# Gates, in_proj and ssm_out as 32x32 tiles in one block of a scan kernel

## The chip, the cores and the metric

The kernel runs on one core of one Trainium2 chip. The metric is the time of one execution on the device, in microseconds. A core has TensorE (PE in the profile; its weight loads are PEld), VectorE (DVE), ScalarE (ACT), GpSimd (POOL) and SyncE (SP), which issues most transfers. Each runs its own list of instructions in order and waits on semaphores for the others. All arithmetic here is in f32.

## The reference

The input is x, 4 images of 128 channels and 96 x 96 points. It is normalized in 32 groups of channels, put through the layer below, and added to the result. The layer reads each image as a sequence of 9216 points in four ways: by rows, by rows backwards, by columns, by columns backwards. Each sequence goes through the same scan, and a 1x1 convolution (fuse_w) joins the four results:

```python
t = _grouped1x1(x, in_proj_w, in_proj_b, G)            # 4 groups of 32 channels -> 512
u, gate = (t[:, :HID], t[:, HID:])                     # 256 each
u = jax.nn.silu(u)
u = depthwise_conv(u, dw_w)                            # 5 taps, 256 channels
s = _conv1x1(u, ssm_in_w)                              # 32 channels each, from 256
a = DMIN + (DMAX - DMIN) * jax.nn.sigmoid(_conv1x1(u, ssm_delta_w, ssm_delta_b))
bb = jnp.tanh(_conv1x1(u, ssm_b_w, ssm_b_b))
cc = jnp.tanh(_conv1x1(u, ssm_c_w, ssm_c_b))
prefix = jnp.cumsum(jnp.log(a), axis=-1)
hst = jnp.exp(prefix) * jnp.cumsum(bb * s * jnp.exp(-prefix), axis=-1)
u = u + _conv1x1(cc * hst + ssm_d[None, :, None] * s, ssm_out_w)
u = _grouped1x1(u * jax.nn.sigmoid(gate), mix_w, mix_b, G)
return _conv1x1(u, out_proj_w, out_proj_b)
```

## The kernel before

**Units.** The work is 8 phases, for each of the 4 images first "V" (columns) and then "H" (rows). A phase runs a sequence and its reverse side by side. It has 6 steps of 16 lines. A step's 1536 points are held as 4 interleaved sets of N = 384 points (p = 0 to 3), so that neighbours along the sequence lie in neighbouring sets. A unit is one set of one direction, and a pair t holds the two directions' units of one set (s = 0 and 1): 24 pairs a phase, 192 in all. `pair(t)` records what the engines do for a pair. The order is written out by hand; no scheduler changes it.

**What a pair does**, by functions:
- `front` (`compute_front`, `in_proj`, `silu`): the grouped projection to u of a pair four ahead (t + 4), as 16 matmuls of 32 rows x 32 columns into four PSUM banks, then a silu per bank. In the second half of a phase the reversed sequence meets the same points, so the silu's results are kept in HBM and loaded again. Fronts are thus computed in pairs with t mod 24 in 20 to 23 and 0 to 7.
- `conv` and `conv_less`: the depthwise convolution of the first 128 channels as banded matmuls, 8 of 128 x 32 and 8 of 64 x 32, then a copy to u. `taps`: the other 128 channels, the first tap on ScalarE and four on VectorE, gathered in PSUM banks 0 and 1.
- `proj`: the projections to s, a, b and c, 16 matmuls of 128 x 32, then tanh and copies on ScalarE and two products on GpSimd. `scan` on VectorE and `outputs` on GpSimd make the value that goes into ssm_out, some pairs later.
- `out_of` (ssm_out): for the pair n = t - 6 (LAG = 6; its first unit is bi), four matmuls of 32 rows x 128 columns into banks 0 to 3. With `under`, ScalarE first lays u into the bank, so that the sum is made in PSUM; in the other pairs VectorE adds u.
- `gate` and `sigmoids`: the gates of pair n, four matmuls of 32 x 128 and four tanh (the factor of a half is folded into weights). The mirrored second half of a phase needs no new gates: they are kept in SBUF (`gates`, two tiles) and HBM (`kept`), and `load_kept` loads them. Gates are computed where n mod 24 is under 12, that is t mod 24 in 6 to 17.
- `gating` on VectorE multiplies, and `accumulate` applies the joined output weight W (w_fin: out_proj, mix and fuse in one, made at the start), 8 matmuls of 128 x 32 per unit; ScalarE copies the bank to `ys`, GpSimd adds it into `acc`.

In the profile an f32 matmul is two MATMUL records and two LDWEIGHTS. All matmuls recorded by the helper `mm` have its line, 134; the full-width gates are line 491, ssm_out line 504.

**Order.** A pair with kept gates runs on TensorE: in_proj, convolution, W (both units), less, ssm_out, projections. A pair with gates and no front: convolution, half of W, less, half of W, gates and ssm_out mixed (`gates_and_out`), projections. Two pairs of a phase have a front and gates, two have neither. TensorE has 8 PSUM banks: 0 to 3 for ssm_out (0 and 1 for the taps before that), and 4 to 7 are handed round among convolution, W, in_proj, gates and projections.

**Statistics.** In V phases, `stats_finish` works out the next image's normalization in pieces, one `next` in some pairs, with a few tiny matmuls (`product`).

**Transfers.** SyncE issues them in program order: the input x_in for fronts (`load_front`) and gates (`load_gate`), kept silus and gates, chunks for the statistics, the output, and the next image into acc.

Of the kernel before, what the change touches and what calls it, by code (L numbers as in the profile page):

```python
# [42 lines left out]
F32 = mybir.dt.float32  # L43
# [4 lines left out]
P = 128  # L48
# [8 lines left out]
R = 4  # L57
# [4 lines left out]
LAG = 6  # L62
# [5 lines left out]
def conv_preact_kernel(  # L68
# [111 lines left out]
    def stats_finish(b):  # L180
# [5 lines left out]

        mv = sp.tile([P, 2], F32, tag="mv", name=f"mv_{b}")
# [5 lines left out]
        nc.vector.tensor_copy(mean, pm[:, 0:1])  # L193
        dev = sp.tile([P, 1], F32, tag="dev", name=f"dev_{b}")
# [12 lines left out]
        nc.vector.tensor_scalar_add(var, pv[:, 0:2], GN_EPS)  # L207
        inv = sp.tile([P, 2], F32, tag="inv", name=f"inv_{b}")
        if b == b0:
            std = sp.tile([P, 2], F32, tag="err", name="std")  # L210
            nc.scalar.activation(std, var, AF.Sqrt)

            nc.scalar.activation(first_table, std[:, 0:1], AF.Silu)
            nc.vector.reciprocal(inv, std)
        else:
            bits = inv.bitcast(I32)
            nc.vector.tensor_single_scalar(bits, var.bitcast(I32), 1, ALU.logical_shift_right)
            nc.vector.tensor_scalar(bits, bits, -1.0, float(0x5F3759DF), ALU.mult, ALU.add)
            err = sp.tile([P, 2], F32, tag="err", name=f"err_{b}")
            for turn in range(3):  # L220
                if turn:
                    yield
                nc.gpsimd.tensor_mul(err, inv, inv)
# [3 lines left out]
        yield  # L227
        wns = sp.tile([P, 2, P], F32, tag="wn", name=f"wn_{b}")
# [16 lines left out]
        else:  # L245
# [3 lines left out]
            nc.vector.tensor_copy(shift, pb[:, 0:1])  # L249
            nc.vector.tensor_scalar_mul(spread, gmask, shift)  # L250
# [4 lines left out]
            nc.vector.tensor_sub(bn[:, 4:8], b_in[:, 4:8], pq[:, 0:4])  # L255
        nc.vector.tensor_scalar_mul(bn[:, 2:4], bn[:, 2:4], 0.5)
# [42 lines left out]

    b0 = phases[0][0]  # L300
# [7 lines left out]
    w_out_fuse = load(fuse, "fuse")  # L308
# [11 lines left out]
    w_mix = w_out_fuse[:, HID + 4 * P :].rearrange("p (j c) -> p j c", j=2)  # L320
# [140 lines left out]
    def in_proj(step, g, s, j, bk):  # L461
        wn = stats[units[step * UB]["b"]][0]
        r = slice(64 * s + 32 * j, 64 * s + 32 * j + 32)
        for c in range(4):
            m, q = (c, g) if j else (g, R - 1 - c if s else c)
            mm(bank(bk), c, wn[r, s, 32 * m : 32 * m + 32], x_in[s][r, q, :], True, True)

    def silu(step, g, s, j, bk):
# [3 lines left out]
            bank(bk)[:, : N + 1],  # L472
            AF.Silu,
# [19 lines left out]

    turning = (6, 0, 2)
# [11 lines left out]

    seeded = set()

    def under(bi, s):

        seeded.add(bi)
        nc.scalar.copy(psum[:, ssm(bi, s) : ssm(bi, s) + 2, :N], us[bi][:, s])  # L512

# [19 lines left out]

    def load_kept(n):
        m = mirror(n)
        if n < NU // 2 - R and m is not None and m < NP // 2 - 2:
            old_gates[n] = gates[m % 2]
            nc.sync.dma_start(old_gates[n], kept[n // NP % 2][m])
# [43 lines left out]
    def gating(bi, s):  # L582
# [3 lines left out]
        if m is None:  # L586
            g = gates[bi // 2 % 2][:, s]
        else:
            g = old_gates.get(bi // 2, gates[m % 2])[:, 1 - s, :, ::-1]
# [29 lines left out]
    def conv_less(i, banks):  # L619
# [10 lines left out]
        else:  # L630
            nc.scalar.copy(us[i][:, :, 0, :], psum[:, b0 : b0 + 2, :N])  # L631

# [291 lines left out]

    def tail():
# [90 lines left out]
    def start():  # L1016
        w_of = wp.tile([P, 4, 2, P], F32, name="w_of")

# [92 lines left out]
    with tc.manual_schedule(  # L1111
# [5 lines left out]
        for t in range(NU // 2):  # L1117
            pair(t)
        tail()
# [81 lines left out]
```

## Time and profile before

| | |
|---|---|
| runs shown | 1810.45, 1811.15, 1817.87 us; median 1811.15 |
| profiled execution, first to last instruction | 1812.7 us |
| TensorE busy | 1788.9 us, 24090 matmul records |
| weight loads | 645.3 us, 24090 |
| VectorE, ScalarE, GpSimd busy | 1446.5, 1567.0, 1432.0 us |
| granted TensorE clock, mean | 0.998 |
| transfers | 321.17 MB, mean 177 GB/s |

The page states for the profiled execution only its span, 1812.7 us; it is 1.55 us above the median of the runs. In a group's row, the line of the kernel, the engine, the operation, what is written and read with its shape and count come first, then busy time and mean ns of one, then the idle time ahead of these instructions and what ended it. In the timeline a row has start, length and count of like instructions that follow each other. In the table of stretches, "(x n)" counts the instructions that run in a stretch, also those that began before it.

### The profile page before, as it was taken

The numbers are of one execution on the slowest core, as the hardware profiler recorded it, in microseconds if no ns is written. First come the engines' busy times: TensorE is split into PE (matmuls) and PEld (weight loads), VectorE is DVE, ScalarE is ACT, GpSimd is POOL, SyncE is SP. The second block draws the span as 40 slices with busy tenths as digits, with TensorE's granted clock in tenths as the row PEclk, the third lists the DMA queues.
The fourth block names the chain that finished last, engine by engine and source line by source line (L and its number), as shares of the span: only waits on it lengthen the run. The fifth ranks groups of instructions, "written<-read, shape, count | busy, mean of one in ns | idle before, by whom it ended". The sixth has DMA issues, their size and how long they took to land.

```text
span 1812.7 us, 56970 instructions
## 1 busy us (share of the span) xinstructions
PE 1788.9 (99%) x24090; PEld 645.3 (36%) x24090; DVE 1446.5 (80%) x1462; ACT 1567.0 (86%) x2750; POOL 1432.0 (79%) x1477
## 2 busy tenths in 40 slices
PE   6999999999999999999999999999999999999998
PEld 3333333333333333333333333333333333333333
DVE  5888878887888887877788888787877878777886
ACT  4988888998888888898988888889888888889975
POOL 3587887778778888788877888778778788887876
PEclk9999999999999999999999999999999999999999
DMA  7655463444975466344696447443477734645434
GB/s 229 183 184 196 149 185 117 163 145 142 305 246 188 159 177 204 102 145 141 204 306 225 159 161 211 138 146 119 160 232 223 249 118 150 192 122 176 148 112 175
DMA packets 148047, 321.17 MB, mean 177 GB/s; under 512 B 14160, under 2 KB 115920, under 8 KB 147792
## 3 DMA queue, kind: packets, MB, share of 16 engines
q1 hardware_dynamic: 147648, 317.48, 54.4%
q8 instruction: 190, 3.11, 0.7%
q14 instruction: 65, 0.53, 0.1%
q10 hardware_dynamic: 144, 0.04, 0.0%
HBM read 185.21 MB, written 132.25 MB: 175 GB/s over the span
## 4 chain that ended last, share of the span: by engine, by line
PE 95%; DMA 2%; DVE 2%; ACT 1%; issue 0%; SPq 0%; DVEq 0%
PE psum L134 82%; PE psum L504 8%; PE psum L491 5%; DVE psum L650 1%; DMA x_in<-in_xs 1%; DMA xs<-in_xr 1%; DMA acc<-in_xr 0%; DVE u L597 0%; DVE u L650 0%; ACT psum L512 0%; PE psum L1035 0%; ACT u L631 0%; SPq L296 0%; ACT ys L757 0%; DVE bn L387 0%
## 5 line engine op out<-in xcount | busy, mean ns | idle before, releaser
L650 DVE SCALAR_TENSOR_TENSOR psum<-sil,small,psum 128x768 f32<-128x768 f32 x576 | 589.0, 1023 | 28.4 <-ACT psum L648 3.4
L597 DVE SCALAR_TENSOR_TENSOR u<-gate,psum 128x768 f32<-128x768 f32 x376 | 350.0, 953 | 273.4 <-ACT u L629 119.0
L134 PE MATMUL psum<-u,w_fin 128*32 128x384 f32 (+1 forms) x6192 | 551.1, 485 | 1.6 <-ACT ys L755 1.2
L134 PE MATMUL psum<-u,main 128*32 128x384 f32 x6144 | 534.7, 489 | 1.5 <-DVE u L650 1.4
L774 POOL TENSOR_TENSOR acc<-ys,acc 128x384 f32<-128x384 f32 x375 | 411.6, 1119 | 24.0 <-ACT ys L757 7.9
L728 POOL TENSOR_TENSOR t<-t,t 64x384 f32<-64x384 f32 (+1 forms) x192 | 237.7, 1238 | 156.9 <-DVE t L722 73.2
L134 PEld LDWEIGHTS psum<-u,w_fin 128*32 128x32 f32 x6192 | 189.3, 109 | 319.6 <-issue 215.3
L134 PEld LDWEIGHTS psum<-u,main 128*32 128x32 f32 x6144 | 181.9, 109 | 324.7 <-issue 197.2
L512 ACT COPY psum<-u 128x768 f32<-128x768 f32 x352 | 277.3, 801 | 17.5 <-DVE u L650 11.5
L134 PE MATMUL psum<-sil,band 128*32 128x384 f32 x3072 | 285.1, 488 | 0.0
L695 POOL TENSOR_SCALAR t<-tm 64x384 f32<-64x384 f32 x191 | 176.9, 926 | 117.3 <-ACT tm L687 97.9
L729 POOL TENSOR_TENSOR t<-t,t 64x384 f32<-64x384 f32 (+1 forms) x192 | 249.1, 1297 | 15.0
L504 PE MATMUL psum<-t,main 32*128 32x384 f32 x1536 | 238.6, 513 | 1.3 <-ACT psum L512 0.6
L648 ACT ACTIVATE psum<-sil,small 128x768 f32<-128x768 f32 x191 | 173.7, 909 | 56.2 <-DVE u L597 48.0
L521 ACT ACTIVATE gate<-psum,bnorm 128x384 f32<-128x384 f32 x384 | 192.2, 584 | 26.5 <-PE psum L491 25.5
L696 POOL TENSOR_TENSOR t<-t,tm 64x384 f32<-64x384 f32 x192 | 195.3, 1017 | 15.3
L650 DVE SCALAR_TENSOR_TENSOR u<-sil,small,psum 128x768 f32<-128x768 f32 x192 | 194.9, 1015 | 7.8
L470 ACT ACTIVATE sil<-psum,bnorm 128x385 f32<-128x385 f32 x384 | 192.6, 585 | 7.1 <-PE psum L134 4.8
L134 PE MATMUL psum<-sil,less 64*32 64x384 f32 x3072 | 168.1, 495 | 0.0
L491 PE MATMUL psum<-x_in,wn 32*128 32x384 f32 x768 | 157.3, 527 | 0.0
L134 PEld LDWEIGHTS psum<-sil,band 128*32 128x32 f32 x3072 | 90.6, 109 | 169.2 <-issue 94.4
L731 POOL COPY t<-t 64x384 f32<-64x384 f32 x187 | 136.8, 731 | 11.9
(103 smaller groups left out, 1480.3 us busy)
## 6 DMA issues: line engine op xcount, KB each, us to landing
sil<-sil SPq DMA_DIRECT2D x128, 770.0 KB, 6.7
kept<-gate SPq DMA_DIRECT2D x80, 768.0 KB, 3.7
gate<-kept SPq DMA_DIRECT2D x76, 768.0 KB, 4.9
x_in<-in_xs SPq DMA_DIRECT2D x192, 96.2 KB, 2.5
out<-acc SPq DMA_DIRECT2D x48, 384.0 KB, 8.2
acc<-in_xr SPq DMA_DIRECT2D x39, 384.0 KB, 6.8
xs<-in_xr SPq DMA_DIRECT2D x72, 192.0 KB, 5.7
x_in<-in_xs SPq DMA_DIRECT2D x46, 192.5 KB, 3.5
```

Of the source, the lines that this page charges most:

```text
L134: nc.tensor.matmul(o[r, : rhs.shape[-1]], lhsT, rhs, start=start, stop=stop, skip_group_check=True)
L470: nc.scalar.activation(sils[step][:, s, j, g, :], bank(bk)[:, : N + 1], AF.Silu, bias=bn[:, 1:2] if j else bn[:, 4 + g : 5 + g],)
L491: nc.tensor.matmul(bank(to)[:, :N], stats[un["b"]][0][r, s, :], x_in[s][r, q, off : off + N], start=True, stop=True)
L504: nc.tensor.matmul(bank(ssm(bi, s) + j)[:, :N], w_so[r, bass.ts(j, P)], z[r, :], start=bi not in seeded, stop=True, skip_group_check=True)
L512: nc.scalar.copy(psum[:, ssm(bi, s) : ssm(bi, s) + 2, :N], us[bi][:, s])
L521: nc.scalar.activation(gv[:, s, j, :], bank(to[2 * s + j])[:, :N], AF.Tanh, bias=bn[:, 2 + j : 3 + j], scale=0.5,)
L597: nc.vector.scalar_tensor_tensor(v, g, 1.0, pz, ALU.add, ALU.mult)
L650: nc.vector.scalar_tensor_tensor(us[i][:, :, 1, :] if k == K - 1 else part, src, w_tap[:, k : k + 1], part, ALU.mult, ALU.add,)
L696: nc.gpsimd.tensor_mul(ta[0:64, p, :], tb[0:64, :], tm[0:64, :])
L728: engine.tensor_mul(ta[0:64, p, r], tb[64:P, r], ta[64:P, p, r])
L729: engine.tensor_add(tb[0:64, r], ta[0:64, p, r], tb[0:64, r])
L774: adder.tensor_add(part, y, part)
```

## The change

From pair 8 on, `pair_of_tiles` takes the place of `pair`. ssm_out and the gates become 32x32 tiles (`out_tile`, `gate_tile`), four times as many matmuls; in_proj is recorded tile by tile. Each pair has one block of two halves, in which 16 tiles of in_proj or of gates alternate with 16 of ssm_out: in the first half j = 1 of the one and unit 0 of the other, in the second j = 0 and unit 1. In each half the 16 tiles are on different places of the 4 x 4 row and column groups.

The gates are made a pair ahead (for n + 1). The first three gates of a phase are made in the pairs t mod 24 = 17, 18, 19 of the phase before, which had neither front nor gates or the last gates; they go through a tile that shares its room with start-up weights, are stored in `kept` and loaded later. Pair 8 makes its own gates apart. Each pair thus has either a front or gates, but for the last seven, which have neither. On TensorE the order is convolution, less, W for both units, block, projections. Unit 0's gating is followed by the next pair's first tap, then unit 1's. u is always laid under the sum. Banks 4 to 7 alternate in two pairs of banks (`cb`, `db`) from pair to pair. The silu and the tanh of the second half are one instruction over two banks (`silu_both`, `tanh_both`), and so is the copy after less (`less_both`). The statistics have more pieces, two a pair.

```diff
+    def in_proj_tile(step, g, s, j, bk, c):
         wn = stats[units[step * UB]["b"]][0]
         r = slice(64 * s + 32 * j, 64 * s + 32 * j + 32)
+        m, q = (c, g) if j else (g, R - 1 - c if s else c)
+        mm(bank(bk), c, wn[r, s, 32 * m : 32 * m + 32], x_in[s][r, q, :], True, True)
...
+    def gate_tile(n, s, j, to, c):
+        un = units[2 * n + s]
+        q, off = gate_at(un)
+        r = slice(64 * (1 - s) + 32 * j, 64 * (1 - s) + 32 * j + 32)
+        mm(bank(to), c, stats[un["b"]][0][r, s, bass.ts(c, 32)], x_in[s][r, q, off : off + N],
+           True, True)
...
+    def out_tile(bi, s, j, c):
+        r = slice(64 * j + 32 * s, 64 * j + 32 * s + 32)
+        mm(bank(ssm(bi, s) + j), c, w_so[r, bass.ds(j * P + 32 * c, 32)], tbs[bi][r, :], False, True)
...
     def load_kept(n):
         m = mirror(n)
+        if n % NP < 3 and NP <= n < NU // 2:
+            nc.sync.dma_start(tile_of(n), kept[n // NP % 2][n % NP])
...
+    def pair_of_tiles(t):
+        i, k, n, end = 2 * t, t % R, t - LAG, NU // 2
+        bi, last = 2 * n, t == end - 1
+        cb, db = ((6, 7), (4, 5))[:: 1 if t % 2 == 0 else -1]
...
+        fronted, gated = fresh(step), None
+        if mirror(n + 1) is None and (n + 1) % NP > 2:
+            gated = n + 1
+            to = tile_of(gated)
+        elif t % NP in (17, 18, 19) and t + LAG + 1 < end:
+            gated = t + LAG + 1
+            to = shared()[:, : 4 * N].rearrange("p (s j n) -> p s j n", s=2, j=2)
...
+        taps(i, (1, 2))
...
+        taps(i, (3, 4))
...
+        conv(i, cb)
+        under(bi, 1)
+        if t > LAG + 2:
+            scale_s(i - 4)
+        less_both(i, cb)
+        recurrence(t)
+        stats_chunks(t)
+        under(bi, 0)
...
+        adds = [accumulate(waiting.pop(0), b, *((nc.vector, True) if last else ())) for b in db]
...
+        for j in (1, 0):
+            for c in range(4):
+                for s in range(2):
+                    if fronted:
+                        in_proj_tile(step, g, s, j, (db, cb)[j][s], c)
+                    elif gated is not None:
+                        gate_tile(gated, s, j, (db, cb)[j][s], c)
+                for e in range(2):
+                    out_tile(bi, 1 - j, e, c)
+
+        if fronted:
+            for s in range(2):
+                silu(step, g, s, 1, cb[s])
+        elif gated is not None:
+            for s in range(2):
+                tanh_one(gated, to, s, 1, cb[s])
+        gating(bi, 0)
+        first_tap(i + 2)
+        gating(bi, 1)
+        if fronted:
+            silu_both(step, g, 0, db[0])
...
+            after_front(step, g)
+        elif gated is not None:
+            tanh_both(gated, to, 0, db[0])
+            if gated % NP < NP // 2 - 2:
+                nc.sync.dma_start(kept[gated // NP % 2][gated % NP], to)
+            for s in range(2):
+                load_gate(2 * gated + s + UB)
+        if t % NP in (14, 15, 16, 17):
+            for s in range(2):
+                load_gate(2 * (t + 10) + s)
...
+            load_kept(n + 2)
...
+        proj(i, cb, True)
...
         start()
-        for t in range(NU // 2):
+        for t in range(LAG + 2):
             pair(t)
+        for t in range(LAG + 2, NU // 2):
+            pair_of_tiles(t)
         tail()
```

More of the change, by code (lines that the diff above doesn't have):

```diff
@@ L227, in stats_finish @@
         yield
+        if b != b0:
+            yield
         wns = sp.tile([P, 2, P], F32, tag="wn", name=f"wn_{b}")
@@ L631, in conv_less, with less_both @@
             nc.scalar.copy(us[i][:, :, 0, :], psum[:, b0 : b0 + 2, :N])
+    def less_both(i, banks):
+        step, p = units[i]["step"], units[i]["p"]
+        sil, k = blocks(step), less_of(p)
+        for g in range(4):
+            for s in range(2):
+                r = less_rows(s, p)
+                mm(bank(banks[s]), g, less[r, p, g, :], columns(step, sil[s][r, g, :], k), False, True)
+        nc.scalar.copy(us[i][:, :, 0, :], psum[:, banks[0] : banks[0] + 2, :N])
     def new_u(i):
```

119 lines of the change are left out of this document (109 added, 10 removed).

## The prediction

> **What bounds the kernel now.** I read the page's engine shares and its chain of waits first, then the table of stretches, then the timeline of TensorE pair by pair.
>
> ```profile
> span 1812.7 us, 56970 instructions
> PE 1788.9 (99%) x24090; PEld 645.3 (36%) x24090; DVE 1446.5 (80%) x1462; ACT 1567.0 (86%) x2750; POOL 1432.0 (79%) x1477
> PE 95%; DMA 2%; DVE 2%; ACT 1%; issue 0%; SPq 0%; DVEq 0%
> ```
>
> TensorE is busy for 99% of the span and makes 95% of the chain that ended last. So a term counts only by what it does to the time between one TensorE stage and the next. The changed pairs are t = 8 to 191. They lie between the start of the projections of t = 7, at 88.31, and that of t = 191, at 1778.10, 184 periods later:
>
> ```profile
> 88.31 0.51 PE L134 MATMUL psum<-u,main 128*32 128x384 f32 x4
> ```
>
> ```profile
> 88.30:1778.10 1689.80, 1687.87 (x22700) 602.51 (x22693) 1360.69 (x1336) 1489.23 (x2607) 1373.92 (x1392) 1.00 0.55 176
> ```
>
> The columns are the length, then busy time and count of PE, PEld, DVE, ACT and POOL, the granted clock (1.00), DMA share and rate. 1689.80 / 184 is 9.18 a pair; ACT has 8.09 of it, POOL 7.47, DVE 7.40. The sum is made against these 1689.80 us; what lies before and after is left as it is. The profiled span is 1.55 above the runs' median of 1811.15, and I put the difference that I find on the median.
>
> Two pairs of the timeline carry the rest. First one with gates and no front, from one projection to the next:
>
> ```profile
> 548.99 2.79 PE L134 MATMUL psum<-u,main 128*32 128x384 f32 x32
> 551.60 1.47 PE L134 MATMUL psum<-sil,band 128*32 128x384 f32 x16
> 552.89 1.47 PE L134 MATMUL psum<-u,w_fin 128*32 128x384 f32 x16
> 554.29 0.88 PE L134 MATMUL psum<-sil,less 64*32 64x384 f32 x16
> 555.10 1.50 PE L134 MATMUL psum<-u,w_fin 128*32 128x384 f32 x16
> 556.52 0.59 PE L491 MATMUL psum<-x_in,wn 32*128 32x384 f32 x2
> ...
> 558.11 2.79 PE L134 MATMUL psum<-u,main 128*32 128x384 f32 x32
> ```
>
> Then one with a front and kept gates:
>
> ```profile
> 501.14 2.79 PE L134 MATMUL psum<-u,main 128*32 128x384 f32 x32
> 503.86 0.94 PE L134 MATMUL psum<-x_in,wn 32*32 32x385 f32 x32
> 504.74 1.50 PE L134 MATMUL psum<-sil,band 128*32 128x384 f32 x16
> 506.05 2.77 PE L134 MATMUL psum<-u,w_fin 128*32 128x384 f32 x32
> 508.75 0.88 PE L134 MATMUL psum<-sil,less 64*32 64x384 f32 x16
> 509.55 0.93 PE L504 MATMUL psum<-t,main 32*128 32x384 f32 x8
> 510.41 2.79 PE L134 MATMUL psum<-u,main 128*32 128x384 f32 x32
> ```
>
> The reader should see that stages follow each other without a gap, and that each pass of a 128-row matmul over its four column tiles takes 2.61 / 8 = 0.33 us (the projections, 16 matmuls of two records each, four at a time). Where the tile form changes, about 0.12 more goes by: the convolution takes 551.60 to 552.89 (1.29) before W of the same form, and W 552.89 to 554.29 (1.40) before the 64-row form. Gates and ssm_out together take 558.11 - 556.52 = 1.59. The front's in_proj takes 0.88, ssm_out alone 0.86, so 1.74 in such a pair.
>
> **The change, part by part.**
>
> *The fixed stages.* The new order is convolution, less, W (both units), block, projections, convolution. From the first timeline: projections before a convolution 2.61; convolution before another form 1.40 (the row of W before less, of the same 16 records); less 0.81; both halves of W 1.29 + 1.42 = 2.71. Together 7.53 a pair, for every pair. A front pair has one form change fewer than before (five became four), a gate pair as many as before (four).
>
> *The block.* It takes the place of 1.59 or 1.74. Every changed pair from t = 8 to 184, 177 of them, gets two times 16 tiles of 32x32: a front or a set of gates, and ssm_out, so that each half covers all four row groups and all four column groups once. One such 16 is shown: in_proj in the front pair.
>
> ```profile
> 503.86:503.95 0.09, 0.09 (x18) 0.09 (x24) 0.09 (x1) 0.08 (x1) 0.00 (x0) 1.00 1.04 222
> 504.20:504.33 0.13, 0.13 (x32) 0.00 (x0) 0.10 (x1) 0.13 (x1) 0.13 (x1) 1.00 0.93 213
> ```
>
> Of the 18 records in the first stretch four are the projections' last; 14 tiles start within 0.09. All 16 second passes have started by 504.33, about 0.35 after their first, and the next form starts 0.41 later, at 504.74. If the second 16 could enter behind the first at once, a block would be 0.88 + 2 x 0.33 = 1.54. Whether they can is the question, as nothing in steady state shows 32 tiles in a row. The start-up does, with 44 matmuls of in_proj on the 16 tiles:
>
> ```profile
> 24.31 2.06 PEld L134 LDWEIGHTS psum<-x_in,wn 32*32 32x32 f32 x62 [1.10 <-DVE bnorm L256]
> 26.66 0.99 PEld L134 LDWEIGHTS psum<-x_in,wn 32*32 32x32 f32 x20 [0.29 <-issue]
> 28.18 0.26 PEld L134 LDWEIGHTS psum<-x_in,wn 32*32 32x32 f32 x6 [0.52 <-issue]
> ```
>
> ```profile
> 26.40:26.55 0.15, 0.15 (x13) 0.00 (x0) 0.02 (x1) 0.15 (x1) 0.00 (x0) 0.50 0.00 0
> 26.89:27.00 0.11, 0.11 (x20) 0.11 (x8) 0.01 (x1) 0.11 (x1) 0.00 (x0) 0.50 0.00 0
> ```
>
> At half clock (0.50) the loads come in three batches, with 0.29 and 0.52 us between them in which they wait for nothing that is shown ("issue"). In 26.40 to 26.55, 13 of the 16 tiles work, none is loaded, and the three idle ones belong to the very matmuls that come next; they get going when older matmuls end, about 26.9. I read this as a window: about 16 f32 matmuls (64 loads and passes) may be in the engine, a new one enters when the oldest has left, and they leave in the order of the program. [...]
>
> By that reading the first 16 fill the window alone, and the second 16 enter singly from when the first matmul has left. A record of this form lasts 0.50 (mean below) and the first's second pass starts at 0.35, so that is about 0.86 after the block's start. From there entry goes at the program's own pace, since nothing could be brought in beforehand: 16 one-column matmuls on 32x32 tiles took 0.43, of which one record is 0.17, so 0.26 / 16 = 0.016 us each.
>
> ```profile
> 22.79 0.43 PE L134 MATMUL psum<-mean,wn 32*32 32x1 f32 x32
> ```
>
> ```profile
> L134 PE MATMUL psum<-x_in,wn 32*32 32x385 f32 x3072 | 96.7, 499 | 0.4 <-DMA x_in<-in_xs 0.4
> L134 PE MATMUL psum<-mean,wn 32*32 32x1 f32 x32 | 0.4, 168 | 0.0
> L512 ACT COPY psum<-u 128x768 f32<-128x768 f32 x352 | 277.3, 801 | 17.5 <-DVE u L650 11.5 <-DVE u L597 3.4
> L648 ACT ACTIVATE psum<-sil,small 128x768 f32<-128x768 f32 x191 | 173.7, 909 | 56.2 <-DVE u L597 48.0 <-DVE u L650 1.5
> L757 ACT COPY ys<-psum 128x384 f32<-128x384 f32 x281 | 130.4, 478 | 16.1 <-PE psum L134 15.9
> L650 DVE SCALAR_TENSOR_TENSOR psum<-sil,small,psum 128x768 f32<-128x768 f32 x576 | 589.0, 1023 | 28.4 <-ACT psum L648 3.4
> L597 DVE SCALAR_TENSOR_TENSOR u<-gate,psum 128x768 f32<-128x768 f32 x376 | 350.0, 953 | 273.4 <-ACT u L629 119.0 <-ACT gate L521 114.9 <-PE psum L504 31.0
> gate<-kept SPq DMA_DIRECT2D x76, 768.0 KB, 4.9
> ```
>
> A block is then 0.86 + 15 x 0.016 + 0.35 (to the last second pass) + 0.41 (to the next form) = 1.86. The ends: 1.54 if all packs; 2.06 if ScalarE holds the second half up by 0.2 (below). I take 1.86, the value of the only stretch in the trace where the tiles had more than 16 matmuls ahead of them.
>
> *The sum.* Changed periods: 177 x (7.53 + 1.86) = 1662.0. The last seven pairs (t = 185 to 191) have neither front nor gates; their block is 16 tiles of ssm_out, 0.88, so 7 x 8.41 = 58.9. Pair 8 first makes its own gates, another burst with its change of form, 1.0. Together 1721.9, against 1689.8: 32 us more. 1811 + 32 = 1843.
>
> *Edits costed at nothing.* Gates a pair ahead take a wait off VectorE's gating (114.9 us on the tanh, in L597's row), and 28 of its adds become ScalarE copies; neither engine is the bound. Each ScalarE write of two banks instead of two writes saves ScalarE time, not TensorE time. ScalarE stays near 8.1 of a 9.4 us period, so it isn't the bound on average. What releases whom inside a pair: the first half of the block ends, VectorE gates unit 0 (0.95), ScalarE writes the first tap (0.91), VectorE adds four taps (4 x 1.02), ScalarE lays u under the sum (0.80), and the next block may start. That is 6.7, counted from about 1.0 after the block's start, against a period of 9.4; the cover is 1.6 us, and if it went, each microsecond over it would cost 177. The scan and statistics stand behind the taps on VectorE's queue and have that room too. The second half's banks are freed by the copy of W's second unit (0.48). W's last pass starts 0.41 before the block and is written by about 0.1 after it starts, so the copy ends near 0.6 and the second half wants the bank at 0.86: a cover of some 0.2, the thinnest. On SyncE's queue the early gates move three stores a phase forward and add three loads, 21 in all, each 4.9 us from issue to landing and asked for two pairs (18.8 us) ahead; the gates' x_in loads, now issued a pair earlier, stand behind at most one store. The extra yields in the statistics put every small product a pair behind the VectorE work that it needs. The shared tile is small arithmetic at the start.
>
> **The rivals.**
>
> *The tiles pack.* If the second 16 enter behind the first without waiting, the block is 1.54: 177 x 9.07 + 58.9 + 1.0 = 1665.3, 25 less, 1787. For it: in_proj shows 16 tiles at full rate. Against it: the two pauses in the loads at start-up, though at half clock. [...] The point from which it decides: the block must be under 1.68 for any gain, as (1689.8 - 58.9 - 1.0) / 177 - 7.53 = 1.68.
>
> *A shorter stop.* If the second half starts only when the first has left, but then at the first's pace, the block is 2 x 0.88 = 1.76: 14 us more, 1825.
>
> *ScalarE late in the second half.* If the copy of W's second bank ends 0.2 beyond the 0.86, as it would where one more ScalarE copy stands ahead of it, the block is 2.06, 35 us more than forecast: 1878. For it: in a pair ScalarE has three copies of the 128x768 kind (0.80) and two of 0.48 ahead of the block's second half, in a fixed order. Against it: 1.3 us of slack a pair.
>
> That the products don't become tiles is no rival: 736 of ssm_out's 768 become 2944 and 376 of the gates' 384 become 1504, so TensorE's records go from 24090 to 30762.
>
> **How the numbers follow.** Window with slow entry, 0.52 (1830 to 1860); the shorter stop, 0.14; ScalarE late, 0.16; packing, 0.14; something dearer than all these, 0.04. The likeliest gives 1843. Leaving out the packing and the dearest case, the range is 1798 to 1884. About 9 us, 0.5%, is what can be told from no change: faster than that needs a block under 1.63 (packing, 0.15 with its edge), within it 1.63 to 1.73 (the shorter stop's lower edge, 0.07), slower the rest, 0.78.
>
> **What would show it.** In the profile after: 64 records of 32x32 tiles in each pair between W and the projections, the next projection 1.86 after the first of them, and a stop in the weight loads before the second 32; the period 9.39 in gate and front pairs alike; convolution 1.40, less 0.81, W 2.71. A block at 1.54 proves the window wrong; one over 1.9 with the stop ended by "ACT ys" proves ScalarE late. Gaps ahead of less, W or the projections, of which I forecast none, would make the fixed 7.53 wrong.

## The result and the profile after

The changed kernel takes 1895.5 us (median of 4 runs, 1886.20 to 1898.93) against 1811.14 for the kernel before on the same chip. The ratio is 1.0452, with a 95% interval of 1.0422 to 1.0482. The forecast was 1843, in a range of 1798 to 1884: the direction was right, the size too small, and the measured time lies 12 us above the range.

The page is of the slowest of the four runs (1898.93 us, mean granted clock 0.992; the fastest, 1886.20, had 0.997), so what is read from it lies near the upper end. The changed kernel's span, busy times, queues, chain that ended last, and a group of instructions:

```profile
span 1897.2 us, 70215 instructions
PE 1852.9 (98%) x30762; PEld 679.6 (36%) x30762; DVE 1403.2 (74%) x1434; ACT 1568.5 (83%) x2515; POOL 1444.2 (76%) x1477
...
q1 hardware_dynamic: 150672, 334.00, 57.1%
q8 instruction: 243, 3.98, 0.9%
...
PE 96%; issue 1%; DMA 1%; ACT 0%; DVE 0%; SPq 0%; DVEq 0%
...
L134 PE MATMUL psum<-u,main 128*32 128x384 f32 x6144 | 544.7, 492 | 14.1 <-issue 12.0
```

The queues' rows are packets, MB and share of the 16 engines. The same rows of the kernel before, where they were not shown yet:

```profile
q1 hardware_dynamic: 147648, 317.48, 54.4%
q8 instruction: 190, 3.11, 0.7%
...
L134 PE MATMUL psum<-u,main 128*32 128x384 f32 x6144 | 534.7, 489 | 1.5 <-DVE u L650 1.4
```

TensorE is still the bound, and no other engine is nearer to it. Two things are new. The idle time ahead of the projections rose from 1.5 to 14.1 us, of which 12.0 is "issue": TensorE waited for nothing that the profile shows. And queue q8 (kind "instruction") moved 243 packets of 16 KB in place of 190. Its packets come in step with what TensorE has executed (below): it carries TensorE's own program, and 30762 matmul records need more of it than 24090 (253 and 254 records to a packet, with as many weight loads counted in).

The pairs run from the projections of t = 7 to those of t = 191 in 1771.9 us, where the forecast had 1721.9 and the kernel before 1689.8. A steady pair, and one with a stop:

```profile
503.10 1.15 PE L134 MATMUL psum<-u,w_fin 128*32 128x384 f32 x12
504.18 0.51 PE L134 MATMUL psum<-x_in,wn 32*32 32x385 f32 x2
...
504.62 0.50 PE L134 MATMUL psum<-t,main 32*32 32x384 f32 x2
504.86 0.69 PE L134 MATMUL psum<-x_in,wn 32*32 32x385 f32 x2
505.06 0.52 PE L134 MATMUL psum<-t,main 32*32 32x384 f32 x2
...
505.66 0.50 PE L134 MATMUL psum<-t,main 32*32 32x384 f32 x2
506.08 0.53 PE L134 MATMUL psum<-u,main 128*32 128x384 f32 x4
```

```profile
516.51 1.79 PE L134 MATMUL psum<-u,main 128*32 128x384 f32 x20
518.12 1.13 PE L134 MATMUL psum<-sil,band 128*32 128x384 f32 x9
519.52 0.85 PE L134 MATMUL psum<-sil,band 128*32 128x384 f32 x7 [0.26 <-issue]
520.30 0.88 PE L134 MATMUL psum<-sil,less 64*32 64x384 f32 x16
521.11 2.79 PE L134 MATMUL psum<-u,w_fin 128*32 128x384 f32 x32
...
525.73 0.85 PE L134 MATMUL psum<-u,main 128*32 128x384 f32 x6
529.19 3.14 PE L134 MATMUL psum<-u,main 128*32 128x384 f32 x24 [2.61 <-issue]
```

In the first, the block lasts from 504.18 to 506.08, 1.90 (forecast 1.86). Its first 16 matmuls have had both passes started by 504.64. By the single records, one of the second 16 enters at 504.86 (the row has merged its two passes), and the next, the eighteenth of the block, only at 505.04, 0.87 after the start (forecast 0.86); from there on a record starts about every 0.017. In the second, TensorE stops twice, in the middle of the convolution and in the middle of the projections, with operands long there: in each case matmuls of the same kind had run before the stop.

What the transfers did between these two stops, as the queues' rows (packets, MB, share of the 16 engines) for 518.2 to 526.6 and then for 526.6 to 527.8:

```profile
q1 hardware_dynamic: 1175, 2.29, 103.9%
...
q1 hardware_dynamic: 207, 0.34, 75.1%
q8 instruction: 1, 0.02, 5.3%
```

For 8.4 us the data filled the engines (the share is a sum of the packets' times, so it can pass 100%) and no piece of TensorE's program came; one came at 526.69, had landed at 527.70 by its packet's own record, and TensorE went on at 529.19. Every one of the 15 stops that the stretch shows, 21.1 us in all, ends so: 1.2 to 1.5 us after a piece has landed. (One of them, 0.65 us in pair 148, the profile puts down to ScalarE, the others to "issue".) And where two stops follow each other, as here, they lie some 250 records apart, matmuls and weight loads together (five times). The whole kernel has 61524 such records in 243 pieces, 253 a piece, so that is one piece of the program.

A long pause between two pieces is not enough: one of 11.4 us brought no stop. What counts is how far TensorE has come. When a piece's transfer begins, it has run, beyond 253.2 records for each piece before, 220 in the median, but 385 to 437 ahead of the 15 stops; only one other piece began that late.

Pairs are named below by the projections that end them. Sixteen of them (23, 24, 49, 52, 53, 56, 71, 96, 97, 100, 101, 119, 144, 145, 148, 149) hold 37.0 us beyond the usual 9.436. That is more than the 21.1 of the stops: a stop is counted only once the last matmul has left, and after four of them the clock goes to half for 3.41 us, as here (the columns end with granted clock, DMA share and GB/s):

```profile
526.50:529.20 2.70, 0.09 (x5) 0.01 (x3) 2.52 (x4) 1.27 (x2) 0.21 (x1) 1.00 0.86 268
530.20:533.60 3.40, 3.40 (x28) 1.27 (x24) 2.79 (x2) 0.58 (x1) 1.81 (x1) 0.50 0.98 336
```

### The profile page after: what moved, and what is told of

It is laid out like the page before. It is cut to its first block, busy times and chain, and to the rows that moved or that the text cites. A ratio compares the mean times of both kernels' runs of the same rounds, so it can differ in the third digit from the quotient of the medians.

```text
span 1897.2 us, 70215 instructions
## 1 busy us (share of the span) xinstructions
PE 1852.9 (98%) x30762; PEld 679.6 (36%) x30762; DVE 1403.2 (74%) x1434; ACT 1568.5 (83%) x2515; POOL 1444.2 (76%) x1477
## 3 DMA queue, kind: packets, MB, share of 16 engines
q1 hardware_dynamic: 150672, 334.00, 57.1%
## 4 chain that ended last, share of the span: by engine, by line
PE 96%; issue 1%; DMA 1%; ACT 0%; DVE 0%; SPq 0%; DVEq 0%
PE psum L134 95%; DMA xs<-in_xr 1%; DMA acc<-in_xr 0%; PE psum L1209 0%; PE psum L541 0%; PE psum L1224 0%; DVE psum L721 0%; PE psum L521 0%; SPq L307 0%; PE psum L1216 0%; DVE u L659 0%; ACT sil L491 0%; ACT psum L553 0%; ACT t L776 0%; DVE bn L405 0%
## 5 line engine op out<-in xcount | busy, mean ns | idle before, releaser
L134 PE MATMUL psum<-u,main 128*32 128x384 f32 x6144 | 544.7, 492 | 14.1 <-issue 12.0
L134 PE MATMUL psum<-u,w_fin 128*32 128x384 f32 (+1 forms) x6192 | 535.8, 487 | 1.0 <-ACT ys L826 0.5
L134 PE MATMUL psum<-x_in,wn 32*32 32x385 f32 (+1 forms) x6080 | 357.8, 497 | 0.7 <-DVE sil L449 0.7
L134 PE MATMUL psum<-t,main 32*32 32x384 f32 x5888 | 354.8, 492 | 2.9 <-issue 2.8
L799 POOL TENSOR_TENSOR t<-t,t 64x384 f32<-64x384 f32 (+1 forms) x192 | 237.7, 1238 | 123.0 <-DVE t L793 108.3
L553 ACT COPY psum<-u 128x768 f32<-128x768 f32 x380 | 306.3, 806 | 10.3 <-DVE u L659 4.7
L800 POOL TENSOR_TENSOR t<-t,t 64x384 f32<-64x384 f32 (+1 forms) x192 | 297.4, 1549 | 15.1
L134 PEld LDWEIGHTS psum<-x_in,wn 32*32 32x32 f32 x6080 | 145.8, 103 | 191.6 <-ACT ys L828 59.4
L828 ACT COPY ys<-psum 128x384 f32<-128x384 f32 x281 | 135.2, 481 | 57.2 <-PE psum L134 57.1
L702 ACT COPY u<-psum 128x768 f32<-128x768 f32 x184 | 147.0, 799 | 14.9 <-PE psum L134 10.7
L134 PEld LDWEIGHTS psum<-sil,band 128*32 128x32 f32 x3072 | 100.9, 110 | 159.8 <-issue 120.9
```

Source lines behind the costliest of these rows:

```text
L134: nc.tensor.matmul(o[r, : rhs.shape[-1]], lhsT, rhs, start=start, stop=stop, skip_group_check=True)
L702: nc.scalar.copy(us[i][:, :, 0, :], psum[:, banks[0] : banks[0] + 2, :N])
L799: engine.tensor_mul(ta[0:64, p, r], tb[64:P, r], ta[64:P, p, r])
L800: engine.tensor_add(tb[0:64, r], ta[0:64, p, r], tb[0:64, r])
L828: nc.scalar.copy(ys, y)
```

## The experiments

A time without an interval is that of one run, or the middle of two that are named. The kernel before took 1809.6 to 1812.1 us (medians) on the chips used.

**Tiles alone, in the order of before.** In the kernel before, ssm_out and the gates become tiles:

```diff
-        nc.tensor.matmul(bank(to)[:, :N], stats[un["b"]][0][r, s, :], x_in[s][r, q, off : off + N],
+        for c in range(4):
+            mm(bank(to), c, stats[un["b"]][0][r, s, bass.ts(c, 32)], x_in[s][r, q, off : off + N],
...
-        nc.tensor.matmul(bank(ssm(bi, s) + j)[:, :N], w_so[r, bass.ts(j, P)], z[r, :],
+        for c in range(4):
+            mm(bank(ssm(bi, s) + j), c, w_so[r, bass.ds(j * P + 32 * c, 32)], z[r, :],
```

> The kernel before, with its order and transfers, but ssm_out and the gates as 32x32 tiles in place (four for one). Theory A: where gates and ssm_out stand together the 32 tiles take 1.90 instead of 1.59, in about 94 pairs, 29 us; ssm_out alone stays near 0.88; the records rise to about 31000, and TensorE stops for its program as in the changed kernel, 20 to 40 us: 1860 to 1880. Theory B: the tiles cost the 29 us alone, with no stops ended by 'issue': 1842.

Measured: 1849.4 us. The timeline of a gate pair's block:

```profile
543.53 0.55 PE L134 MATMUL psum<-x_in,wn 32*32 32x384 f32 x8
...
545.44 0.53 PE L134 MATMUL psum<-u,main 128*32 128x384 f32 x4
```

The block takes 1.91, as in the new order, and gate pairs take 9.43 for 9.11. The tiles bring the cost of the block with them, whatever the order. By the single records the eighteenth matmul enters at 544.40, 0.86 after the start, here too. Stops are few, about 3 us in three pairs (96, 97, 149), though 244 pieces of program are fetched.

**The block with fewer tiles.** In the changed kernel the first half has no ssm_out (that part of the sum is left out):

```diff
-                for e in range(2):
+                for e in range(0 if j else 2):
                     out_tile(bi, 1 - j, e, c)
```

> The changed kernel without ssm_out of unit 0, the 8 tiles of it in the first half of the block (its product is left out of the sum); the second half keeps its 16 tiles and its banks. Window of 16 matmuls: only the last eight must wait for others to leave, so the last enters 7 x 0.016 after 0.86 and the block takes 0.97 + 0.35 + 0.41 = 1.73 (1.77 scaled to the measured 1.90). Rival (the second half waits for ScalarE's copy of W's second bank): its 16 tiles start as late as before and the block stays at 1.90. Stops ended by 'issue' are fewer than in the changed kernel, as the program is shorter by 1400 matmuls.

Measured: 1828.9 us, a period of 9.276, so a block of 9.276 - 7.53 = 1.75:

```profile
523.44 1.18 PE L134 MATMUL psum<-x_in,wn 32*32 32x385 f32 x19
524.12 0.51 PE L134 MATMUL psum<-t,main 32*32 32x384 f32 x2
524.13 0.52 PE L134 MATMUL psum<-x_in,wn 32*32 32x385 f32 x2
524.15 0.51 PE L134 MATMUL psum<-t,main 32*32 32x384 f32 x2
524.16 0.65 PE L134 MATMUL psum<-x_in,wn 32*32 32x385 f32 x2
524.32 0.52 PE L134 MATMUL psum<-t,main 32*32 32x384 f32 x2
```

```profile
523.58 0.48 ACT L828 COPY ys<-psum 128x384 f32<-128x384 f32 x1 [0.23 <-PE psum L134]
```

The first run holds the eight matmuls of the first half and the first of the second, of two records each, and one record more: the next matmul of the second half, at 524.11, 0.67 after the start. No matmul of the first half uses its place in the array, but it writes the bank from which ScalarE copies W's second unit, until 524.06. So here the rival, ScalarE's copy, does hold the second half for a time. After this matmul and seven more comes a pause, from 524.16 to 524.31, and behind it the rest enters one by one. It comes before the eighteenth matmul counted from the block's start, as in the block of 32 (504.86 to 505.04) and in the old order (544.23 to 544.40), and in all three the eighteenth enters 0.03 to 0.04 after the end that the profile gives for the block's first matmul. So the bound is read, from these three blocks, as one on the number of matmuls under way. It also sets the length, and the copy does not: the last first pass starts 0.99 after the block's start, its second pass 0.34 later and the next form 0.41 after that. In the changed kernel the copy has ended by 504.79, 0.25 before the eighteenth enters. Four pairs hold 5.1 us of longer time.

**Wide forms in the new order.** ssm_out, the gates and the first half of in_proj become 32 x 128 again:

```diff
+    def in_proj_wide(step, g, s, bk):
+        wn = stats[units[step * UB]["b"]][0]
+        r = slice(64 * s + 32, 64 * s + 64)
+        nc.tensor.matmul(bank(bk)[:, : N + 1], wn[r, s, :], x_in[s][r, g, :], start=True, stop=True)
...
-                    if fronted:
-                        in_proj_tile(step, g, s, j, (db, cb)[j][s], c)
...
+            for s in range(2):
+                if fronted and j:
+                    in_proj_wide(step, g, s, (db, cb)[j][s])
+                elif gated is not None:
+                    gate(2 * gated + s, s, j, (db, cb)[j][s])
+            for e in range(2):
+                out_of(bi, 1 - j, e)
+            if fronted and not j:
+                for c in range(4):
+                    for s in range(2):
+                        in_proj_tile(step, g, s, j, db[s], c)
```

> The changed kernel, but ssm_out, the gates and the j = 1 half of in_proj as matmuls of 32 rows x 128 columns again (one in place of four tiles); only the j = 0 half of in_proj stays 32x32. Order, early gates and banks are as in the changed kernel. Theory A (the window of 16 matmuls makes the block 1.90 us, and the 17 long pairs, 42 us, are TensorE waiting for its own program, which has grown by a quarter): the block is about 1.6 us in gate and front pairs, the period 9.12 to 9.15, the records fall to about 23000, the long stops of TensorE ended by 'issue' are gone; time about 1800. Theory B (the long pairs come from the new transfers, the early gates and their loads): the block shrinks in the same way, but the stops of some 40 us stay; about 1840. If a change between 32x128 and 32x32 inside a half drains the array, front pairs are 0.2 longer, 17 us more in either case.

Measured: 1859.4 us, ratio 1.0279 (1.0262 to 1.0296). Gate pairs take 9.11 (block 1.59, as before), front pairs 9.83; in them the form changes inside the block, whose rows go on to the projections at 502.79:

```profile
500.50 0.59 PE L492 MATMUL psum<-x_in,wn 32*128 32x385 f32 x2
...
501.99 0.88 PE L134 MATMUL psum<-x_in,wn 32*32 32x385 f32 x16
502.79 0.53 PE L134 MATMUL psum<-u,main 128*32 128x384 f32 x4
```

That block is 2.29, 1.49 of it up to the start of the 32x32 tiles and 0.80 from there, and 84 front pairs that are 0.7 longer are 59 us, the miss against the expected 1800. How much of it the change of form alone costs no run shows. The transfers are those of the changed kernel, with 183 pieces of program, and there is no stop after pair 8: with a short program the new transfers bring none.

**The order without tiles.** ssm_out and the gates 32 x 128, and in_proj's 16 tiles in one burst ahead of ssm_out:

```diff
+        if fronted:
+            for j in (1, 0):
+                for s in range(2):
+                    for c in range(4):
+                        in_proj_tile(step, g, s, j, (db, cb)[j][s], c)
+            for s in range(2):
+                for e in range(2):
+                    out_of(bi, s, e)
```

> The changed kernel with its order, early gates and banks, but ssm_out and the gates 32x128 as before; in_proj stays 16 tiles in its own burst, with ssm_out behind it. Order alone, without the 32 tiles: gate pairs as in the run with wide forms, 9.11; front pairs 7.53 + 0.88 + 0.86 = 9.27; pair 8 some 3 us dearer; no stops ended by 'issue', as the program is as short as before. Stretch from the projections of pair 7 to those of pair 191: 93 x 9.11 + 84 x 9.27 + 58.9 + 3 = 1688, as before (1690): 1809 to 1813. Rival (the early gates and their loads cost of themselves): 20 us or more above.

Measured: 1891.0 us, ratio 1.0446 (1.0428 to 1.0463), far from what was expected. Gate pairs take 9.11, front pairs 10.22, and no stop for the program is left. Rows of TensorE, then of ScalarE:

```profile
498.77 1.52 PE L134 MATMUL psum<-x_in,wn 32*32 32x385 f32 x32
500.22 0.93 PE L541 MATMUL psum<-t,main 32*128 32x384 f32 x8
501.08 2.79 PE L134 MATMUL psum<-u,main 128*32 128x384 f32 x32
```

```profile
498.12 0.58 ACT L826 ACTIVATE ys<-psum,b_fin 128x384 f32<-128x384 f32 x1
498.91 0.48 ACT L828 COPY ys<-psum 128x384 f32<-128x384 f32 x1 [0.21 <-PE psum L134]
```

in_proj takes 1.45 to the next form, where it took 0.88 before. By the single records, 12 of its 16 tiles start at 498.77 to 498.85 and four at 499.44: they write the bank from which ScalarE copies W's second unit, until 499.39. In the changed kernel that bank is wanted only in the block's second half.

**ssm_out first.** The same with the two swapped:

```diff
         if fronted:
+            for s in range(2):
+                for e in range(2):
+                    out_of(bi, s, e)
             for j in (1, 0):
...
-            for s in range(2):
-                for e in range(2):
-                    out_of(bi, s, e)
```

> The changed kernel's order without tiles for ssm_out and the gates, with ssm_out now ahead of the 16 in_proj tiles instead of behind them. Theory: the 1891.0 us of the other order came from in_proj's last four tiles, which waited 0.67 us for ScalarE's copy of W's bank (ended 499.39, tiles from 499.44) and held ssm_out behind them; with 0.86 us of ssm_out in between that copy is done, and the front pairs fall from 10.22 to 9.25 to 9.45 (7.53 of fixed stages, 0.86 of ssm_out, 0.87 to 1.0 of in_proj), the gate pairs stay at 9.11: 1808 to 1822 us, without TensorE stops. Rival (the new order itself delays the front pairs, by silu or by gating): front pairs of 9.7 or more, over 1840 us.

Measured: 1870.5 us, ratio 1.0334 (1.0302 to 1.0366). The wait for the copy is gone, and another has come, so that front pairs take 9.94:

```profile
493.40 0.93 PE L541 MATMUL psum<-t,main 32*128 32x384 f32 x8
494.25 1.00 PE L134 MATMUL psum<-x_in,wn 32*32 32x385 f32 x32
495.81 0.53 PE L134 MATMUL psum<-u,main 128*32 128x384 f32 x4 [0.56 <-ACT sil L491]
```

The projections take a bank that the silu still reads. So the rival holds here: with in_proj as one burst, front pairs take 0.6 to 0.9 more than the 9.30 of the kernel before, and 0.56 (here) or 0.57 (above) of that is one wait for ScalarE. That the new order would be free without tiles is not shown by any run.

**No loads of kept gates.** The changed kernel without its 97 loads of kept gates; the gating of those pairs then uses gates that are not theirs:

```diff
     def load_kept(n):
+        return
```

> The changed kernel without the loads of kept gates (97 transfers of 768 KB are left out; the gating then uses whatever gates stand in the tile). All matmuls are as in the changed kernel, with block 1.90 and period 9.44. Theory A: the pieces of TensorE's program come sooner with 22% less traffic beside them, so most of the stops go, 1860 to 1875, but not all need go. Theory B: the stops go with the loads, 1853. If neither traffic nor loads matter, 1895.

Measured: 1854.6 us. The queues:

```profile
q1 hardware_dynamic: 136704, 257.71, 42.5%
q8 instruction: 243, 3.98, 0.9%
```

The program is as long as in the changed kernel, and the period 9.436, but no pair after pair 8 is longer. The stretch is 1733.0 for 1771.9. That is the time of theory B; what speaks against transfers alone is the run with wide forms.

**Only the early gates' 21 loads taken out:**

```diff
-        if n % NP < 3 and NP <= n < NU // 2:
-            nc.sync.dma_start(tile_of(n), kept[n // NP % 2][n % NP])
```

> The changed kernel without the 21 loads of early gates alone (the first three gates of a phase are then stale in their tile); the other 76 loads of kept gates stay. Theory C (a stop needs both, the longer program and a stretch in which the transfers fill the DMA engines): the long pairs at t mod 48 = 4, 5 and 8, where the early gates are loaded, go, about 16 us; those at t mod 48 = 23, 24, 0 and 1, where mirrored gates and silus are loaded, stay, about 20 us; 1875 to 1885. If the early loads alone are the trigger (their transfers push those of the next pairs back): all stops go, 1853. If the program's length alone is: nothing goes, 1895.

Measured: 1879.3 us, a time as expected, but not in the pairs that were expected. Fifteen pairs hold 26.0 us in place of 37.0, mostly the same pairs, and the longest are 53 and 101 (5.4 and 4.9), t mod 48 = 5, which were to go. The other 76 loads, which the kernel before has too, suffice for most of the long pairs.

**Small matmuls in the kernel before**, 17 in each pair from t = 7:

```diff
+        if t > LAG:
+            for n in range(17):
+                mm(psum[:, 3, 500:501], n % 4, w_fin[:, 0, 0, 0:32], w_fin[:, 0, 0, 0:1], True, True)
```

> The kernel before, with 17 one-column matmuls of 128x32 (they are read by nothing) after the projections in each pair from t = 7: TensorE's program grows to about that of the changed kernel, all else stays. At 0.016 us each they take 0.27 a pair, 50 us. Theory A: beside that TensorE stops for its program, in gaps ended by 'issue', for 20 to 40 us; 1880 to 1900. Theory B: no such gaps, 1862.

Measured: 1880.1 us, in the range of theory A, but not by stops. The stretch grows by 62.7 to 1752.5, 0.34 a pair, so the small matmuls cost some 0.02 each and not 0.016. With 238 pieces only three pairs, 50, 146 and 147, are longer, by 2.4 us. So a longer program with the transfers of before brings few stops.

**Longer program without more tiles.** The kernel of wide forms, with W and less in matmuls of 192 columns (the cut of less is shown with the next run):

```diff
-                mm(py, c, w_fin[:, bu["dir"], j, 32 * c : 32 * c + 32], bu["v"][:, j, :],
-                   j == 0, j == 1)
+                for h in range(2):
+                    q = bass.ts(h, N // 2)
+                    mm(py[:, q], c, w_fin[:, bu["dir"], j, 32 * c : 32 * c + 32],
+                       bu["v"][:, j, q], j == 0, j == 1)
```

> The kernel with wide forms (32x128 for ssm_out, the gates and half of in_proj; 1859.4 us, no TensorE stops) in which every matmul of W and of the convolution's less is cut into two of 192 columns: the same products, the same transfers of 337.5 MB, no 32x32 tile more, but some 31900 matmul records in place of 23082 and so about as much of TensorE's program to fetch as the changed kernel (243 pieces). Theory C (TensorE waits for its own program where the transfers leave the DMA engines no room): the stops of 0.5 to 2.8 us come back, in the pairs where the changed kernel has them (t mod 48 of 0, 1, 4, 5, 8, 23, 24); pairs longer than the median of their kind by over 0.4 us hold together 20 to 45 us, some of them followed by 3.41 us at half clock. Rival (the stops come from the 32x32 tiles or their waits, not from the program's length): fewer than 5 us of stops. The cuts themselves may lengthen each pair by 0 to 0.6 us: 1859 to 1970 us on one core by the rival, 1880 to 2010 by theory C, so the verdict is read from the stops and not from the time.

Measured: 1889.1 us, ratio 1.0437 (1.0407 to 1.0467), with front pairs of 9.98. 254 pieces were fetched, and no stop over 0.15 us came after pair 8. One pair, the 100th, is 0.75 longer: a piece landed at 975.05, and the projections went on at 976.39, before the last matmuls had ended, so that it is not counted as a stop. Theory C, that a long program and full engines are enough, fell as it stood: the front pairs' transfers had more time here than in the changed kernel, but the engines were full all the same (shares of 0.93 to 1.02 from 510 to 522).

**The same two cuts with shorter pairs**, in the kernel whose first half has no ssm_out (that part of the sum is left out here too): less alone, then less and W.

```diff
-                mm(bank(banks[s]), g, less[r, p, g, :], columns(step, sil[s][r, g, :], k), False, True)
+                col = columns(step, sil[s][r, g, :], k)
+                for h in range(2):
+                    q = bass.ts(h, N // 2)
+                    mm(bank(banks[s])[:, q], g, less[r, p, g, :], col[:, q], False, True)
```

> The kernel without unit 0's ssm_out tiles in the first half (1828.9 us, period 9.276, 219 pieces of TensorE's program, stops of 2.1 us in the steady pairs; that part of the sum in ssm_out is still left out) with the convolution's less cut into matmuls of 192 columns: 16 more matmul records and 16 more weight loads a pair, some 242 pieces, the same transfers, the same 32x32 tiles, and about 0.06 us more a pair (0.94 for 0.88 at the cut less). What the run with wide forms and 254 pieces left open is whether program length brings the stops when the pairs are as short as in the changed kernel (there the front pairs took 9.98 us, here 9.34). Theory C (a late piece of the program stops TensorE where the transfers fill the engines): stops of 12 to 30 us, each ending 1.2 to 1.5 us after a piece has landed; 1850 to 1880 us. Rival (the stops hang on the number of 32x32 tiles in the block): stops of 2 us as without the cut; 1838 to 1843 us.

> The same with W cut into matmuls of 192 columns too: some 288 pieces, another 0.09 us a pair (9.43). Theory C: more stops than with less alone, 25 to 60 us; 1880 to 1930 us. Rival (number of 32x32 tiles): stops of 2 us; 1854 to 1862 us.

Measured: 1839.1 us (1836.27 and 1841.86) and 1871.9 us (1865.51 and 1878.28). With 242 pieces and a period of 9.34 no pair is longer; with 290 and 9.43, eleven pairs hold 18.8 us. The first is what the rival expected, the second refutes it, since the tiles are the same in both; but theory C's 12 to 30 and 25 to 60 us did not come either. Pieces against microseconds in long pairs: 219, 5.1; 242, 0; 290, 18.8. Their number alone doesn't set the loss either.

**The borders shifted.** The changed kernel with 32 one-column matmuls, once, ahead of pair 8's convolution:

```diff
+        if t == LAG + 2:
+            for m in range(32):
+                mm(psum[:, 3, 500:501], m % 4, w_fin[:, 0, 0, 0:32], w_fin[:, 0, 0, 0:1], True, True)
         conv(i, cb)
```

> The changed kernel with 32 one-column matmuls put once ahead of pair 8's convolution: 128 records, half a piece of TensorE's program and some 0.8 us, after which the program of every pair, its time of 9.436 us and every transfer are as in the changed kernel, but the borders between the pieces fall half a piece (some 3.8 us of work) elsewhere in the pairs. Runs with 219, 238, 242, 243, 244, 254 and 290 pieces had stops of 2, 3, 0, 27 (42 with what follows them), 4, 0 and 12 us, so the number of pieces alone doesn't set them. Theory D (a stop comes where a border falls due while the transfers have the engines, so the place of the borders decides): the long pairs are others than (8, 23, 24, 49, 52, 53, 56, 71, 96, 97, 100, 101, 119, 144, 145, 148, 149) in more than half, and their excess over 9.436 differs from 42 us by more than 10; 1855 to 1885 us, or 1908 and more. Rival (the pairs' own instructions and transfers decide): the same pairs in at least 12 of 17, excess 37 to 47 us, 1890 to 1902 us.

Measured: 1870.6 us (median of 4 runs, 1868.61 to 1873.68), ratio to the kernel before 1.0341 (1.0324 to 1.0359). More work made the kernel 24.9 us faster. From its page, and from its timeline:

```profile
q1 hardware_dynamic: 150672, 334.00, 55.9%
q8 instruction: 243, 3.98, 0.8%
...
L134 PE MATMUL psum<-u,main 128*32 128x384 f32 x6144 | 539.3, 490 | 3.9 <-issue 3.4
```

```profile
948.33 0.85 PE L134 MATMUL psum<-sil,band 128*32 128x384 f32 x8 [0.55 <-issue]
957.52 3.14 PE L134 MATMUL psum<-u,main 128*32 128x384 f32 x20 [2.14 <-issue]
```

Transfers, pieces and the usual period (9.435) are the same. Six pairs are longer (50, 51, 54, 98, 99, 146), none of the sixteen among them, and they hold 11.2 us. The two profiles differ by 23.7 us in the stretch (1748.2 for 1771.9) and by 6.6 in the start, which no edit touches: there the clock is at half for 10.24 us in the one and not at all in the other. So theory D holds: which stops come, and how much they cost, hangs on where the borders between the pieces fall against the bursts of transfers. In the other runs each cut or tile also moved the borders, which may be why the number of pieces ordered nothing; that was not tested, and how a border and a burst must lie to each other for a piece to be late was not worked out.

## Why the prediction was right and wrong

The stretch came out 50.0 us over the forecast (1771.9 against 1721.9). Term by term:

*The block: right.* 1.90 for 1.86, with the second 16 matmuls, but for the first of them, entering one after the other from 0.87 on. The old order gave 1.91, and 24 matmuls 1.75. The fixed stages stood: 9.436 - 1.90 = 7.53. The 0.046 by which a pair is longer makes 8.1 us over 176 pairs. The pause before the eighteenth matmul, in three runs, agrees with the estimate of about 16 under way; no run shows that the bound counts loads and passes, 64 of them, or that matmuls leave in the order of the program.

*The rivals.* The tiles did not pack, and the block was not 1.76. ScalarE was not late: in the pair whose block starts at 523.82, the copy of W's second unit ended 0.62 after, where the forecast had 0.6 and a want at 0.86:

```profile
523.96 0.48 ACT L828 COPY ys<-psum 128x384 f32<-128x384 f32 x1 [0.66 <-PE psum L134]
```

That thin cover held; the order without tiles showed what it hides (0.57 a front pair).

*Pair 8: mis-sized.* Its own gates were priced at 1.0, as a burst with its change of form. The pair took 14.0, 4.6 over a usual one. The convolution waits for ScalarE to empty the banks of these gates:

```profile
96.33 1.21 PE L134 MATMUL psum<-sil,band 128*32 128x384 f32 x8 [1.78 <-ACT gate L563]
```

and from 96.7 on the clock is at half for 3.41 us. That is 3.6 of the 50.0. Without the half clock (the run without the early gates' loads) the pair took 12.4.

*The step that failed: "Edits costed at nothing".* It priced the early gates' 21 loads by SyncE's queue alone, and the sum had no term for TensorE's program. Records rose by 28% and pieces of program from 190 to 243, and beside more transfers (334.00 MB on q1 for 317.48) some pieces came late. This is 37.0 of the 50.0; with 8.1 and 3.6 that leaves 1.3 in small delays. That TensorE stops for its program is shown: each stop ends 1.2 to 1.5 after a piece lands, stops in a row are one piece apart, and moving the borders moved all of them to other pairs. That they need the transfers is shown by the run without kept gates (257.71 MB on q1), where none is left. Of the 37.0 the 21 early loads carry some 11 (37.0 - 26.0) by one profile of each kernel; four runs of the changed kernel lie 12.7 apart, so this share is rough.

Some 24 us of the result are then a matter of place, which nothing in the prediction could have told: with the borders half a piece elsewhere the same kernel takes 1870.6 and would have been inside the range, by luck and with the same step missing. With no long pair at all, as the run without kept gates has it, it would be near 1855: the forecast's 1843, the 8.1 of the pairs, and some of pair 8. On no reading does the change gain, for the tiles cost the block 1.90 in place of 1.59 or 1.74, and the convolution, less and W in a row save too little: the run without kept gates, which has no stop in the stretch, takes 1733.0 in it for 1689.8, 43 us more. None of the versions run was faster than the kernel before.

## What to carry to other kernels

Price a group of small tiles by how many matmuls may be in the engine at once, not only by the places of the array: here the eighteenth f32 matmul waited for the first, to 0.87 us after the block's start. Instructions can cost their fetch too: here 243 pieces of program for 190, beside more transfers, came with 37.0 us in sixteen long pairs, while 238 pieces beside the transfers of before came with 2.4. Where an edit multiplies the instructions of the engine that is the bound, look at the instruction queue's packets and at the transfers' share of the engines in each stretch, not over the span. And when the bound engine shows "issue" in its chain, shift its program by a few idle instructions before you explain a difference of one or two per cent by the edit itself: here 32 of them made 24.9 us, 1.3%.

## What was not expected

TensorE's program is fetched during the execution, in pieces of 16 KB (243 packets on q8, 0.9% of the time of the 16 DMA engines, where the data's q1 has 57.1%); with the engines full (103.9%) two pieces in a row began 10.1 and 9.5 us after the one before, where 7.9 is the median. The forecast had no term for this, and the sixteen long pairs hold 37.0 us.

Adding 32 matmuls to a kernel took 24.9 us off its median time.

In the changed kernel's trace, stops of 1.78 to 2.81 us were followed by 3.41 us at half clock (five times), stops of 1.92 and less also by none.
